# One feed-forward norm moved along the slots of an interleaved transformer stack

## The chip, the cores and the metric

The kernel runs on one core of a Trainium2 chip. The time is the device time of one execution in microseconds (us), the median of several runs. The core has five engines that work side by side, each through its own list of instructions in order: TensorE (PE in the profile; PEld is its weight loads), VectorE (DVE), ScalarE (ACT), GpSimd (POOL) and SyncE (SP, which here issues the DMA transfers). An instruction that needs another engine's result waits for a semaphore, and everything behind it on its engine waits too. Matmul results land in PSUM, of which this kernel's pools take eight banks of 128 x 512 floats.

## The reference

The computation is four residual blocks on x of 4 x 512 x 128: a linear attention, a stack of six transformer layers, another attention and a gated feed-forward. The change lies in the stack. One of its layers is:

```python
for i in range(DEPTH):                       # DEPTH = 6
    x = attn_layer(shift_tokens(x), Wqkv[i], q_scale[i], k_scale[i], Wo[i]) + x
    x = ffn_layer(shift_tokens(x), ln_g[i], ln_b[i], W1[i], b1[i], W2[i], b2[i]) + x

def ffn_layer(x, g, bln, W1, b1, W2, b2):
    mu = x.mean(-1, keepdims=True)
    var = ((x - mu) ** 2).mean(-1, keepdims=True)
    xn = (x - mu) / jnp.sqrt(var + 1e-05) * g + bln
    hg = xn @ W1 + b1
    a, gate = jnp.split(hg, 2, -1)
    return a * jax.nn.gelu(gate, approximate=False) @ W2 + b2
```

The attention has 16 heads of 64 and looks at windows of 32 queries and 64 keys; q and k are scaled to unit length and rotated. The feed-forward's hidden width is 341.

## The kernel before, in words

**Steps and slots.** The stack is cut into 48 steps: 6 layers x 4 batches (512 tokens each) x 2 halves of the heads (8 heads each). A step has four slots, one for each pair of heads, so there are 192 slots with scores, and some before and behind for filling and draining. The loop at the end of the stack runs over the slots `s`, and its body is a list written out by hand: each call appends its instructions to the engines' lists in just this order. In one slot the list has work of several steps at once: the scores of the present step (`here`), the projections of the step 2.5 steps ahead (`rot`), the transposes of k one step ahead (`turn`), the values half a step ahead (`val`), the weighted sums three slots behind and the output projection four slots behind (`back`).

**A plain slot, engine by engine.** TensorE: eight mask matmuls (L443) and 32 score matmuls (L453) into a pair of banks of which there is one; first projection of q or k (`pp`, L307); four transposes of k into a bank (`tp`, L387); output projection (L521); second projection (L307); weighted sums (L513); values (`pv`, L420). VectorE: maximum of the scores (L460) and `top` (L463), rotation products of the first projection (L318), sums of squares (L343), transposes of the probabilities (`blocks`, L488), products of the second projection, transpose of q (`qb`, L396), reciprocal (L478). ScalarE: four exponentials (L70, `pr`), square of the first projection (L329), copy of k's transposes (L388), four more exponentials, then copies of the weighted sums (L737) and values (L424) and the square of the second projection (L329). GpSimd: rotation sums (L339), normalised probabilities (L479), scaled k (L374), copies in place of the transposed probabilities (L502, L503). The next slot's scores may overwrite the score banks once the second four exponentials have read them.

**PSUM.** Three banks with the tag `mm` serve all of `pp`, `tp`, `pv` and the feed-forward's `pt`, `px`, `pg`, `pa` and `py`. They are handed out in the list's order, each to the next taker, as they come free. A projection's bank is free when both its readers, the rotation product (L318) and the square (L329), are done; the square is ordered behind the rotation product.

**The feed-forward.** It is cut into numbered parts, and a group (one layer, one batch) starts every eight slots. Part p of group g is due in slot `8 g + LATE[p - 1]`; `parts(s, (...))` in the list calls those of its parts that are due. There are 24 groups, g = 1 to 24. Slot numbers modulo 8 say therefore which parts a slot has:

- part 1 (L532): adds the attention's output to the residual stream z, on VectorE
- part 2 (L539, L543): four transposes of z into `pt`, copied by ScalarE to `xt`
- part 3 (L548 to L552): statistics of `xt`: four bn_stats, four bn_aggr, and the variance plus 1e-5 into `rs`, all on VectorE
- part 14 (L570 to L573): root and offset: `rs` to the power -0.5, and `off` as minus mean times `rs`, on GpSimd
- part 4 (L555): four products on ScalarE, `xt` times `rs` plus `off`, in place
- part 5 (L562, L564): four transposes of `xt` back into `px`, and gain and offset by ScalarE into `xg`
- part 6 (L578): gate matmuls into three banks `pg` and their gelu, which needs another table on ScalarE (loaded at L66)
- parts 7 and 8 (L589, L593): the other half of W1, times the gelu
- parts 9 and 15 (L599, L606): the matmuls with W2 into `py`, and their addition to z on VectorE
- parts 10 to 13: the residual of the whole block after the last layer

In slots with part 6 the copies L737 and L424 are made by VectorE and not by ScalarE.

Of the kernel before, what the change touches and what calls it, by code (L numbers as in the profile page):

```python
# [31 lines left out]
def sandwich(ctx: ExitStack, tc: tile.TileContext, a: dict, out: bass.AP):  # L32
# [254 lines left out]
    with tc.tile_pool(name="f0", bufs=2) as work, \  # L287
# [38 lines left out]
        def squares(k, j):  # L326
            o = proj[k]
            sq = o["sq"][j] = work.tile([P, S], F32, tag="ln_sd", name="sq")
            nc.scalar.activation(sq, o["pp"], AF.Square)  # L329
# [73 lines left out]
        def place_q(k, n):  # L403


            o = proj[k]
            if n == 0:
                o["qT"] = work.tile([P, 4, 4, 4, 32], F32, name="qT")
            for f in range(4):
                nc.sync.dma_start(  # L410
                    out=o["qT"][32 * f : 32 * f + 32, n], in_=o["qb"][32 * n : 32 * n + 32, f]
                )
# [21 lines left out]
        def score(k, p):  # L434


            o = proj[k]
            sc = scp.tile([P, 2, S], F32, tag="sc", name="sc")
            scores = o["sc"] = sc[:, :, 0 : 4 * KW].rearrange("p e (j k) -> p e j k", k=KW)
            for w in range(4):  # L440
                for e in range(2):
                    rows = slice(64 * e, 64 * e + 64)
                    nc.tensor.matmul(  # L443
                        sc[32 * w : 32 * w + 32, e, 0 : 4 * KW],
                        lhsT=identb[rows, 64 * e : 64 * e + 32], rhs=mask[rows, int(w == 0)],
                        start=True, stop=False, skip_group_check=True,
                    )
            for j in range(4):
                for w in range(4):
                    q0 = j * P + w * WIN  # L450
                    for e in range(2):
                        rows = slice(64 * e, 64 * e + 64)
                        nc.tensor.matmul(  # L453
                            scores[32 * w : 32 * w + 32, e, j, :],
                            lhsT=o["qT"][rows, w, p, j, :],
                            rhs=o["kT"][rows, p, q0 : q0 + KW],
                            start=False, stop=True, skip_group_check=True,
                        )
            raw = sc[:, 0, 4 * KW : 4 * KW + 8].rearrange("p (e j) -> p e j", e=2)
            nc.vector.tensor_reduce(raw, scores, AX.X, ALU.max, negate=True)  # L460
            top = o["top"] = work.tile([P, 2, 4], F32, name="top")
            o["rq"] = o["rn"][:, 0, :, 2 * p : 2 * p + 2]
            nc.vector.tensor_tensor(top, raw, o["rq"].rearrange("p j e -> p e j"), ALU.mult)  # L463
            o["pr"] = work.tile([P, 2, 4, KW], F32, name="pr")
            o["den"] = work.tile([P, 2, 4], F32, name="den")
# [54 lines left out]
        def output(i, c, t, py):  # L520
            nc.tensor.matmul(py, lhsT=ws[i]["wo"][:, c, :], rhs=t, start=(c == 0), stop=(c == 7))  # L521
# [1 line left out]


        ff = {}
        LATE = (3, 4, 4, 5, 7, 7, 8, 9, 13, 14, 15, 16, 17, 4, 13)

        def ff_part(i, b, part):
            w, zb = ws[i], z[b]
# [85 lines left out]
        def residual(b, part):  # L615
            if not res:
                t = wp.tile([P, 3 * S], F32, tag="wqkv0", name="res")
                res.update(y=t[:, 0:S], sd=t[:, S : 2 * S])
            y, sd = res["y"], res["sd"]
            if part == 1:  # L620
                for rows, cols in halves:
                    nc.gpsimd.tensor_copy(y[rows, :], z[b][rows, cols])
            elif part == 2:
                pc = mm.tile([P, S], F32, tag="mm", name="pc")
                nc.tensor.matmul(pc, lhsT=cent, rhs=y, start=True, stop=True)
                nc.scalar.activation(sd, pc, AF.Square)
                nc.vector.tensor_copy(y, pc)
            elif part == 3:
                pv = mm.tile([P, S], F32, tag="mm", name="pv")
                nc.tensor.matmul(pv, lhsT=mean_w, rhs=sd, start=True, stop=True)  # L630
                table_act(sd, pv, AF.Ln, bias=eps)
                table_act(sd, sd, AF.Exp, scale=-0.5)
            elif part == 4:
                nc.vector.tensor_tensor(y, y, sd, ALU.mult)
                nc.gpsimd.tensor_tensor(x[b], x[b], y, ALU.add)

        def inside(s, ahead):

            k, q = divmod(s + ahead, 4)
            return (k, q) if 0 <= k < len(steps) else None  # L640

        def parts(s, some):
            for part in some:
                g, left = divmod(s - LATE[part - 1], 8)
                if left or not 1 <= g <= DEPTH * NB:
                    continue
                if part < 10 or part > 13:
                    ff_part(*divmod(g - 1, NB), part)
                elif g > NB * (DEPTH - 1):
                    residual((g - 1) % NB, part - 9)  # L650
# [29 lines left out]
        with tc.manual_schedule():  # L680
            for s in range(-10, LAST + max(LATE) + 1):
                here, rot, before, flip = (inside(s, n) for n in (0, 10, 9, 9))
                fold, place, turn, val = (inside(s, n) for n in (6, 5, 4, 2))
                first = fold and fold[1] == 0

                copy = nc.scalar.copy
                if s % 8 == LATE[5] % 8 and LATE[5] < s:
                    copy = nc.vector.tensor_copy
                if place:
                    place_q(*place)  # L690
                if here:
                    score(*here)
                parts(s, (2, 5, 7, 8))
                if rot:
                    project(rot[0], 2 * rot[1])
                if here:
                    exponentials(here[0], 0)
                if rot:
                    rotate(rot[0], 2 * rot[1])
                    squares(rot[0], 2 * rot[1])  # L700
                if before:
                    squared(before[0], 2 * before[1] + 1)
                if turn:
                    turn_k(*turn)
                parts(s, (9,))
                back = inside(s, -4)
                if back:
                    i, b, hf = steps[back[0]]
                    c = 4 * hf + back[1]
                    if c == 0:  # L710
                        ff["py"] = pyp.tile([P, S], F32, name="py")
                    output(i, c, attn, ff["py"])
                if s - 1 in fresh:
                    by_keys[s - 1] = by_key(fresh.pop(s - 1))
                parts(s, (1, 3, 15))
                if s - 2 in by_keys:
                    in_place(*by_keys[s - 2])
                if rot:
                    squared(rot[0], 2 * rot[1])
                    rotated(rot[0], 2 * rot[1])  # L720
                if first:
                    guarded(fold[0])
                parts(s, (4,))
                if rot:
                    project(rot[0], 2 * rot[1] + 1)
                if here:
                    exponentials(here[0], 1)
                if first:
                    norms(fold[0])
                back = inside(s, -3)  # L730
                if back:
                    av = weighted(*back, by_keys.pop(s - 3)[0])
                if rot:
                    rotate(rot[0], 2 * rot[1] + 1)
                if back:
                    attn = work.tile([P, S], F32, tag="attn", bufs=1, name="attn")
                    copy(attn.rearrange("p (j h c) -> p j h c", j=4, h=2), av)  # L737
                if val:
                    value(*val, copy)
                if rot:  # L740
                    squares(rot[0], 2 * rot[1] + 1)
                if flip:
                    flip_q(*flip)
                if rot:
                    rotated(rot[0], 2 * rot[1] + 1)
                if here:
                    fresh[s] = normalise(here[0])
                if first:
                    refined(fold[0])
                if fold:  # L750
                    normed(*fold)
                parts(s, (14, 6, 10, 11, 12, 13))
                if here:
                    weights(*divmod(s, 32))
# [6 lines left out]
    with tc.tile_pool(name="f1w", bufs=1) as gp, tc.tile_pool(name="a1w", bufs=1) as wp, \  # L761
# [242 lines left out]
        parts = [(b, q, i) for b in range(NB) for q in range(2) for i in range(5)]  # L1004
# [195 lines left out]
```

## Time and profile before

| | us |
|---|---|
| median of 3 runs | 2001.5 (1999.19 to 2002.53) |
| the profiled execution | 2002.56 |
| its span, first to last instruction | 2000.9 |
| first scores of slot 0 | 127.5 |
| first scores of slot 191 | 1562.6 |

| engine | share of the span, busy |
|---|---|
| VectorE | 81% |
| ScalarE | 80% |
| GpSimd | 77% |

The stack is 72% of the span, and the granted TensorE clock in it is 1.00 (560 to 1500 us). Within that stretch of 940 us TensorE is busy for 916, VectorE for 841, GpSimd for 822 and ScalarE for 814 us: four engines are close to full. In such a kernel a share says little. What counts is which engine ends a slot, and that differs from slot to slot, since the feed-forward's parts fall into different slots. In the timeline rows the first number is the start in us from the start of the span, the second the length; `x4` after a row means that four instructions in a row are merged, and brackets give the engine's idle time before it and what ended it.

### The profile page before, as it was taken

To read this page: it belongs to the slowest core of one execution; us is meant where nothing else is said; L and a number is where in the kernel's file an instruction comes from. 1 tells how busy PE (TensorE), PEld (TensorE's weight loads), DVE (VectorE), ACT (ScalarE), POOL (GpSimd) and SP (SyncE) were. 2 spreads that over 40 slices of the span, in tenths; PEclk is the share of its full clock that TensorE was granted. 3 is DMA by queue.
4 is the path that set the end of the run, shared out by engine and by line. 5 is a ranking of instruction groups with operands and counts; after the bars stand their busy time and mean duration, and the time that the engine had idled before them with its cause. 6 is when DMAs were issued, how large, how long until landed. Compare 5 with 4: busy or idle time off the path is not lost.

```text
span 2000.9 us, 75927 instructions
## 1 busy us (share of the span) xinstructions
PE 1811.9 (91%) x30648; PEld 950.5 (48%) x30648; DVE 1625.4 (81%) x2561; ACT 1603.8 (80%) x4645; POOL 1547.9 (77%) x2026
## 2 busy tenths in 40 slices
PE   6779899999999999999999999999998868878868
PEld 3235455555555555555555555555555423323323
DVE  3698788888988888988888998889995369889833
ACT  3558788888888889888888888888888639989953
POOL 1289898888988889888898888888886338878850
PEclk8999999999999999999999999999999978889889
DMA  3023443344433444334434345333333110000000
GB/s 99 1 68 96 124 106 77 95 111 113 107 91 86 108 115 112 94 80 118 130 85 99 96 102 131 89 90 96 91 93 95 35 46 1 1 0 1 1 0 21
DMA packets 98892, 155.27 MB, mean 78 GB/s; under 512 B 29552, under 2 KB 56944, under 8 KB 93936
## 3 DMA queue, kind: packets, MB, share of 16 engines
q1 hardware_dynamic: 98544, 150.43, 29.5%
q8 instruction: 243, 3.98, 0.9%
q14 instruction: 105, 0.86, 0.2%
HBM read 23.44 MB, written 1.05 MB: 12 GB/s over the span
## 4 chain that ended last, share of the span: by engine, by line
PE 52%; DVE 16%; ACT 12%; POOL 7%; SPq 5%; issue 4%; DMA 3%; POOLq 0%; DVEq 0%; ACTq 0%
PE pp L307 10%; PE av L513 6%; PE pv L420 6%; PE sc L453 5%; PE py L521 5%; ACT pr L70 4%; PE pa L589 4%; PE pg L578 3%; DVE t L318 3%; DVE la L899 2%; DVE lb L897 2%; PE tp L387 2%; ACT xt L555 2%; POOL r L339 2%; ACT lb L70 2%
## 5 line engine op out<-in xcount | busy, mean ns | idle before, releaser
L70 ACT ACTIVATE pr<-sc,top,rn 128x64 f32<-128x64 f32 x1536 | 604.9, 415 | 99.8 <-DVE top L463 44.0
L339 POOL TENSOR_TENSOR r<-t 128x512 f32<-128x512 f32 x384 | 486.2, 1275 | 154.7 <-DVE t L318 134.2
L318 DVE TENSOR_TENSOR t<-pp,tab 128x1024 f32<-128x1024 f32 x384 | 467.9, 1219 | 39.5 <-PE pp L307 31.3
L307 PE MATMUL pp<-wqkv,z 128*128 128x512 f32 x768 | 410.6, 618 | 12.4 <-ACT sq L329 8.1
L70 ACT ACTIVATION_READ_ACCUMULATOR pr<-sc,top,rn 128x1 f32 x1536 | 329.6, 215 | 0.0
L329 ACT ACTIVATE sq<-pp 128x512 f32<-128x512 f32 x384 | 233.7, 609 | 89.3 <-DVE t L318 85.2
L343 DVE TENSOR_REDUCE ss<-sq 128x8 f32<-128x512 f32 x384 | 256.3, 668 | 3.4 <-ACT sq L329 1.1
L513 PEld LDWEIGHTS av<-pT,ve 64*64 64x64 f32 x6144 | 164.7, 134 | 154.5 <-POOL pT L502 46.4
L907 POOL TENSOR_TENSOR lb<-lb,la 128x2048 f32<-128x2048 f32 x40 | 182.5, 4563 | 53.2 <-issue 35.3
L420 PE MATMUL pv<-wqkv,z 128*128 128x512 f32 x384 | 217.0, 647 | 4.0 <-ACT sq L329 4.0
L479 POOL TENSOR_TENSOR pr<-pr,den 128x512 f32<-128x512 f32 x192 | 200.6, 1045 | 23.9 <-DVE den L478 23.8
L460 DVE TENSOR_REDUCE sc<-sc 128x8 f32<-128x512 f32 x192 | 131.4, 684 | 99.3 <-PE sc L453 98.7
L513 PE MATMUL av<-pT,ve 64*64 64x32 f32 x6144 | 197.0, 222 | 7.9 <-DMA qT<-qb 6.8
L374 POOL TENSOR_TENSOR r<-r,rn 128x512 f32<-128x512 f32 x192 | 200.3, 1043 | 3.8
L307 PEld LDWEIGHTS pp<-wqkv,z 128*128 128x128 f32 x768 | 134.1, 191 | 145.3 <-issue 106.4
L521 PE MATMUL py<-attn,wo 128*128 128x512 f32 x384 | 198.4, 598 | 1.5 <-ACT attn L737 1.5
L513 PE MATMUL av<-pT,vn 64*64 64x32 f32 x6144 | 193.2, 219 | 0.0
L453 PE MATMUL sc<-kT,qT 64*32 64x64 f32 x12288 | 171.1, 223 | 11.8 <-issue 11.8
L503 POOL COPY pT<-blocks 32x256 f32<-32x256 f32 x384 | 151.9, 396 | 22.3
L513 PEld LDWEIGHTS av<-pT,vn 64*64 64x64 f32 x6144 | 165.6, 135 | 0.2
L453 PEld LDWEIGHTS sc<-kT,qT 64*32 64x32 f32 x12288 | 154.6, 105 | 12.9 <-issue 12.7
L502 POOL COPY pT<-blocks 32x256 f32<-32x256 f32 x384 | 149.9, 390 | 11.0 <-issue 2.9
(195 smaller groups left out, 3270.4 us busy)
## 6 DMA issues: line engine op xcount, KB each, us to landing
qT<-qb SPq DMA_DIRECT2D x768, 64.0 KB
ve<-vn SPq DMA_DIRECT2D x48, 768.0 KB
pT<-blocks SPq DMA_DIRECT2D x768, 32.0 KB
wqkv<-in_f_wqkv SPq DMA_DIRECT2D x36, 256.0 KB
ve<-vn SPq DMA_DIRECT2D x48, 192.0 KB
tab<-in_rot SPq DMA_DIRECT2D x12, 256.0 KB
wo<-in_f_wo SPq DMA_DIRECT2D x6, 512.0 KB
ve<-vn SPq DMA_DIRECT2D x48, 64.0 KB
```

The source lines that it names most:

```text
L70: done = nc.scalar.activation(out, in_, func, **kw)
L307: nc.tensor.matmul(pp, lhsT=z[b][:, WIN + t * P : WIN + (t + 1) * P], rhs=ws[i]["qkv", hf][:, n * S : (n + 1) * S], start=True, stop=True,)
L318: nc.vector.tensor_tensor(t12, o["pp"].rearrange("p (h d) -> p h d", d=DH0).unsqueeze(1) .to_broadcast([P, 2, 8, DH0]), ws[i][f"tab{n}"][: ...
L329: nc.scalar.activation(sq, o["pp"], AF.Square)
L339: nc.gpsimd.tensor_tensor(r, t1, t2[:, :, ::-1, :], ALU.add)
L343: nc.vector.tensor_reduce(o["ss"][:, n, t, :], o["sq"].pop(j).rearrange("p (h d) -> p h d", d=DH0), AX.X, ALU.add,)
L374: nc.gpsimd.tensor_tensor(v, v, o["rn"][:, 1, t].unsqueeze(2).to_broadcast([P, 8, DH0]), ALU.mult)
L420: nc.tensor.matmul(pv, lhsT=z[b][:, WIN + t * P : WIN + (t + 1) * P], rhs=ws[i]["qkv", hf][:, 2 * S :], start=True, stop=True,)
L453: nc.tensor.matmul(scores[32 * w : 32 * w + 32, e, j, :], lhsT=o["qT"][rows, w, p, j, :], rhs=o["kT"][rows, p, q0 : q0 + KW], start=False, ...
L479: nc.gpsimd.tensor_tensor(o["pr"], o["pr"], o["den"].unsqueeze(3).to_broadcast([P, 2, 4, KW]), ALU.mult)
L513: nc.tensor.matmul(av[64 * e : 64 * e + 64, h, 64 * j + 32 * c : 64 * j + 32 * c + 32], lhsT=vs[c][rows, j, (2 * p + e) * DH0 : (2 * p + e ...
L521: nc.tensor.matmul(py, lhsT=ws[i]["wo"][:, c, :], rhs=t, start=(c == 0), stop=(c == 7))
```

## The change

Two parts of the feed-forward's norm get a later slot, four get another place in the list:

| part | slot modulo 8 | place in the list |
|---|---|---|
| 3, statistics | 4, now 5 | behind part 15 (was before it; 15 is due in this slot too) |
| 14, root and offset | 4, now 5 | unchanged: the end of GpSimd's list for the slot |
| 4, products | 5, now 6 | behind the square of the second projection, at the end of ScalarE's list for the slot; was ahead of the second projection and the second four exponentials |
| 5, transposes back and `xg` | 7, unchanged | behind k's transposes and part 9; was ahead of the first projection and the first four exponentials |

Nothing is added to the program or taken from it; the same instructions stand in another order. `xt` has one buffer, as before, and is now in use for one slot longer in its unscaled form.

```diff
-        LATE = (3, 4, 4, 5, 7, 7, 8, 9, 13, 14, 15, 16, 17, 4, 13)
+        LATE = (3, 4, 5, 6, 7, 7, 8, 9, 13, 14, 15, 16, 17, 5, 13)
...
-                parts(s, (2, 5, 7, 8))
+                parts(s, (2, 7, 8))
                 if rot:
                     project(rot[0], 2 * rot[1])
...
                 if turn:
                     turn_k(*turn)
-                parts(s, (9,))
+                parts(s, (9, 5))
...
-                parts(s, (1, 3, 15))
+                parts(s, (1, 15, 3))
...
                 if first:
                     guarded(fold[0])
-                parts(s, (4,))
                 if rot:
                     project(rot[0], 2 * rot[1] + 1)
...
                 if rot:
                     squares(rot[0], 2 * rot[1] + 1)
+                parts(s, (4,))
                 if flip:
                     flip_q(*flip)
```

## The prediction

> **What bounds the kernel now.** I read the page first: the busiest row, and then, since busy shares are averages, the list of waits and the timeline of one period of the stack.
>
> ```profile
> PE 1811.9 (91%) x30648; PEld 950.5 (48%) x30648; DVE 1625.4 (81%) x2561; ACT 1603.8 (80%) x4645; POOL 1547.9 (77%) x2026
> PE sc L443 <- ACT pr L70: 31.1, 46, 3.2
> ACT xt L555 <- POOL off L573: 21.7, 23, 3.1
> ```
>
> TensorE works 91% of the span. A slot, measured from the first mask matmul (L443) to the next slot's, has these medians over slots 24 to 183, by slot number modulo 8 ("class"): 7.12, 7.94, 6.24, 6.33, 7.35, 9.29, 6.22, 9.42 us for classes 0 to 7. A plain slot is 6.22 us of TensorE without a gap, so most slots are TensorE's own work. The second row is what is not: 46 times the next slot's scores wait for the exponentials (they reuse the one pair of score banks), 31.1 us in all, once in each class 4 and once in each class 5. That is the most the change could win from this wait.
>
> Class 5 first (slot 69, 647.78 to 657.06), ScalarE's timeline:
>
> ```profile
> 653.82 1.65 ACT L555 ACTIVATE xt<-xt,off,rs 128x128 f32<-128x128 f32 x4 [0.72 <-POOL off L573]
> 655.38 0.39 ACT L70 ACTIVATE pr<-sc,top,rn 128x64 f32<-128x64 f32 x1
> 656.90 0.58 ACT L737 COPY attn<-av 128x512 f32<-128x512 f32 x1
> ```
>
> The four products start only when GpSimd's root and offset are done (0.72 us idle), and the second four exponentials stand behind them: they end at 656.9, and the slot ends just after. TensorE alone would need 6.22 plus the six passes of L599, 2.58 (from 2.29 to 4.87 us in the slot): 8.80 us. The slot took 9.28.
>
> Now VectorE in slots 68 to 70:
>
> ```profile
> 645.73 0.83 DVE L548 BATCH_NORM_STATS2 st<-xt 128x6 f32<-128x128 f32 x4
> 646.88 0.31 DVE L552 TENSOR_SCALAR rs<-mv 128x4 f32<-128x4 f32 x1
> 647.09 0.67 DVE L343 TENSOR_REDUCE ss<-sq 128x8 f32<-128x512 f32 x1
> ...
> 648.82 0.69 DVE L396 STREAM_TRANSPOSE qb<-r 128x512 f32<-128x512 f32 x1
> 649.53 0.64 DVE L460 TENSOR_REDUCE sc<-sc 128x8 f32<-128x512 f32 x1
> ...
> 652.85 1.52 DVE L606 SCALAR_TENSOR_TENSOR z<-py,par,z 64x512 f32<-64x512 f32 x2
> 656.26 0.70 DVE L396 STREAM_TRANSPOSE qb<-r 128x512 f32<-128x512 f32 x1
> 658.06 0.70 DVE L460 TENSOR_REDUCE sc<-sc 128x8 f32<-128x512 f32 x1 [0.81 <-PE sc L453]
> ```
>
> The statistics take 1.36 us of VectorE (645.73 to 647.09). Because of them VectorE enters class 5 with old work: its transpose starts 1.04 us into the slot and the score maximum at 1.75 us. In class 6, where it enters in step, the maximum starts at 1.00 us, after a wait for the scores.
>
> Last, class 7 (slot 71, from 663.28), ScalarE and TensorE:
>
> ```profile
> 664.57 0.61 ACT L329 ACTIVATE sq<-pp 128x512 f32<-128x512 f32 x1
> 665.05 0.79 ACT L564 ACTIVATE xg<-px,par 128x512 f32<-128x512 f32 x1
> 665.84 0.41 ACT L70 ACTIVATE pr<-sc,top,rn 128x64 f32<-128x64 f32 x1
> 667.38 0.60 ACT L329 ACTIVATE sq<-pp 128x512 f32<-128x512 f32 x1
> 664.18 0.66 PE L562 MATMUL px<-ident,xt 128*128 128x128 f32 x4
> 666.13 1.02 PE L521 MATMUL py<-attn,wo 128*128 128x512 f32 x2
> 666.99 1.02 PE L307 MATMUL pp<-wqkv,z 128*128 128x512 f32 x2
> 672.70 0.30 PE L443 MATMUL sc<-mask,identb 64*32 64x256 bf16 x8
> ```
>
> ScalarE has no gap from the end of slot 70's exponentials through these rows, yet TensorE never waits: its second projection (666.99, that is 3.71 us into the slot) needs the PSUM bank that px had, and this is free when xg is done, 2.56 us into the slot.
>
> **The change, part by part.** Each of the 24 feed-forward groups passes once. Of these 23 lie in slots with attention work, the last in the tail.
>
> *Class 4: the statistics leave, 0.* They stand on VectorE behind the maximum. The stall at this slot's end comes from the late maximum, and that from the residual addition (L532) in class 3, which stays.
>
> *Class 5: the products leave, -0.5.* Without them and with VectorE in step, the second exponentials end near 6.2 us, and TensorE sets the slot: 9.28 to 8.80, -0.48; with the class's mean of 9.37 the gain is 0.57. I take 0.5.
>
> *Class 6: the statistics arrive late, +0.65.* They now stand behind L606, which waits for L599, so they cannot start before 6.6 us. What follows moves by 1.36: slot 69's transpose from 8.48 to 9.84 us, in a slot of 8.80, so 1.04 us into class 6. That is the lateness that class 5 has today (648.82 in a slot from 647.78). The maximum then starts at 1.75 and not 1.00 and carries the exponentials with it; they end close to the slot's end today, so the scores of class 7 wait for them. Of 0.75 about 0.1 is slack. Behind the maximum wait both sets of exponentials, and behind these the next scores. The ends are 0 (VectorE catches up) and 0.75.
>
> Here a rule bears on the price. The SBUF page of the Trainium skill ("SBUF — State Buffer", section "Who interferes with whom") has VectorE and GpSimd share a port pair as an exclusive lock: a tensor_scalar in its two-port form waits for GpSimd's whole instruction. The trace agrees:
>
> ```profile
> 662.11 1.03 DVE L351 TENSOR_SCALAR ss<-ss 128x64 f32<-128x64 f32 x1
> 661.82 1.27 POOL L339 TENSOR_TENSOR r<-t 128x512 f32<-128x512 f32 x1
> ```
>
> Both end near 663.1, and L351 is 0.18 us in class 2, where GpSimd isn't in its way. L552 moves with the statistics and has 0.17 to 1.27 us. By its row (median 0.31) it costs what I charged; by the rule's worst case, behind an L339, 1.1 us more, 25 us in all. It should run about 7.7 us into class 5. There GpSimd, rid of root and offsets, should have ended its first rotation sum (today from 655.57, 7.79 us into the slot; less 1.55, plus 1.25 of its own: 7.5) and wait for VectorE's next product; so I take the row.
>
> *GpSimd's root and offsets, 0.* About 1.5 us (652.21 to 653.76) move from behind class 5's to behind class 6's normalisations. Attention's in-place copies behind them serve the next slot's L513, and end about 0.5 us into class 7, where L513 comes after 4.66 us even today. The rotation sums become about 1 us later; the next product on VectorE still finds its buffer free. No DMA is issued by any moved part; SP's queue keeps its order, and its transposes' producers move with their slots.
>
> *Class 7: products ahead of the exponentials, transposes behind k's, +1.82.* The products now follow L329 at the end of class 6's list on ScalarE, in time 1.77 us into class 7 (665.05). Four take 1.56 (653.82 to 655.38). The first exponentials start at 3.33 instead of 2.56, take 1.54 (665.84 to 667.38), and the square of the slot's first projection starts at 4.87. The three general PSUM banks go round, and the fourth taker in a slot gets the first taker's bank. Before, the takers are px, pp, tp, then pp; now pp, tp, px, then pp. So the second projection waits no longer for xg but for that square. In the changed program's instruction list this is the wait it carries. From a square's start to the matmul that waits for it takes 0.66 us:
>
> ```profile
> 137.64 0.60 ACT L329 ACTIVATE sq<-pp 128x512 f32<-128x512 f32 x1
> 138.30 1.12 PE L420 MATMUL pv<-wqkv,z 128*128 128x512 f32 x2 [0.87 <-ACT sq L329]
> ```
>
> So the projection starts at 5.53 instead of 3.71: +1.82, and behind it are L513, L420 and the gate matmuls, all in order. Nothing else is later: px ends by 3.6, output L521 by 4.5, xg (now behind kT) by 6.6, while the gate matmuls come at 8.5; the second exponentials end at 8.15 in a slot of 11.2. The following slots don't give it back; class 0 and 1 are TensorE's own time. Where class 7 starts late anyway (mean 9.63, median 9.42) part is absorbed: -0.15.
>
> *Tail, +3.4.* In the last group nothing is beside the chain. The statistics ended at 1588.36; now they stand behind L606, which ends at 1590.50, plus 1.36: 1591.86.
>
> Sum: 23 x (-0.5 + 0.65 + 1.82 - 0.15) = 23 x 1.82 = 41.9, plus 3.4: +45 us on the profiled execution's 2002.6, so 2047.6. That execution lies 1.1 above the median of 2001.5; forecast **2046.5 us**.
>
> **Rivals.** (a) *The bank is free*: the second projection meets no square, only px's wait. px then ends at 3.58, L521 0.86 later, the projection at 4.44: +0.73 in place of +1.82, and in all 23 x (-0.5 + 0.65 + 0.73 - 0.15) + 3.4 = +20, 2021.5 with the 1.1 to the median. For it: banks could come free in another order; against it: the order of takers above. (b) *Faster*: the class 5 wait goes, and ScalarE takes the products in idle time: 23 x -0.5 + 3.4 = -8, 1993.5. It decides where ScalarE has 1.6 us idle before class 7's first exponentials; there must also be no lateness in class 6. For it are the 0.72 us idle before L555 now; against it the gapless rows from 663.17 on. (c) *VectorE blocked* at L552 in most periods: +25, 2071. (d) *No change*: class 6 at 0 and the bank free make 23 x (-0.5 + 0.73 - 0.15) + 3.4 = +5; with 0.2 us of px's wait hidden too, 2001.5.
>
> **How the numbers follow.** Forecast 0.74, (a) 0.13, (b) 0.06, (c) 0.04, (d) 0.03. Class 6 at 0 gives 2031, class 7 at half its price 2026; class 6 at 0.75 with nothing absorbed gives 2052, and half of (c) on top 2064. With (a) inside, the range is 2018 to 2064; (b), (c) and (d), 0.13, are left out. A difference of 0.2%, 4 us, is about what a measurement here can tell from none. Slower holds forecast, (a) and (c): 0.91; faster 0.06, same 0.03.
>
> **What would show it.** Class 5 at 8.8; class 6 at 6.9 with the maximum at 1.75; class 7 near 11.2, with L307's second start at 5.5 and a wait of PE pp L307 for ACT sq L329, some 0.7 to 1 us in each period, new in the list; "ACT xt L555 <- POOL off" gone. A class 7 that stays below 10 would make it wrong.

## The result, and the profile after

The changed kernel takes 2031.8 us (2028.6 to 2034.7, four runs) where the kernel before, measured beside it, takes 2000.4: a ratio of 1.0164, interval 1.0137 to 1.019. It is 31.5 us, or 1.6%, slower. The profiled execution of the changed kernel took 2028.59 us with a span of 2026.7, so 26 more than the profiled execution of before; it is the shortest of its four runs.

The medians of the slots by class, as in the prediction, over slots 24 to 183:

| class | 0 | 1 | 2 | 3 | 4 | 5 | 6 | 7 |
|---|---|---|---|---|---|---|---|---|
| before, us | 7.12 | 7.94 | 6.24 | 6.34 | 7.35 | 9.29 | 6.22 | 9.42 |
| changed, us | 7.12 | 7.94 | 6.25 | 6.35 | 7.27 | 8.80 | 6.84 | 11.20 |

Three classes differ: one gains half a microsecond and two lose. The busy row and the waits of the changed kernel (who waits, for which tile and line, on whom; us in total, times, the longest) show the causes:

```profile
PE 1823.1 (90%) x30648; PEld 949.8 (47%) x30648; DVE 1618.8 (80%) x2561; ACT 1605.1 (79%) x4645; POOL 1548.7 (76%) x2026
...
PEld pp L307 <- ACT sq L329: 56.2, 38, 2.3
PE sc L443 <- ACT pr L70: 32.9, 52, 2.2
PE pp L307 <- ACT sq L329: 23.1, 27, 1.5
ACT xt L555 <- POOL off L573: 7.5, 1, 7.5
```

The engines' work is what it was: their busy times moved by less than 1%. The wait of L555 for GpSimd, once 23 times, is left in one place, the tail. The wait of L443 for the exponentials is as large as before, 52 times instead of 46: it left the end of class 5 (21 times before, none now) and came up at the end of class 6 (3 times before, 23 now). And the projection L307, whose weight load (PEld) and matmul (PE) waited before for the square L329 19 and 9 times, 21.7 and 8.1 us, now does so 38 and 27 times.

**Class 7** (slot 71, from 661.88 us), timeline of the changed kernel, TensorE:

```profile
661.88 0.30 PE L443 MATMUL sc<-mask,identb 64*32 64x256 bf16 x8 [0.40 <-ACT pr L70]
...
662.77 1.12 PE L307 MATMUL pp<-wqkv,z 128*128 128x512 f32 x2
663.73 0.60 PE L387 MATMUL tp<-ident,r 128*128 128x128 f32 x4
664.16 1.46 PE L562 MATMUL px<-ident,xt 128*128 128x128 f32 x4
665.46 1.02 PE L521 MATMUL py<-attn,wo 128*128 128x512 f32 x2
667.33 1.12 PE L307 MATMUL pp<-wqkv,z 128*128 128x512 f32 x2 [0.84 <-ACT sq L329]
...
673.08 0.30 PE L443 MATMUL sc<-mask,identb 64*32 64x256 bf16 x8
```

and ScalarE in the same slot:

```profile
663.60 1.64 ACT L555 ACTIVATE xt<-xt,off,rs 128x128 f32<-128x128 f32 x4
665.14 0.40 ACT L70 ACTIVATE pr<-sc,top,rn 128x64 f32<-128x64 f32 x1
...
666.67 0.61 ACT L329 ACTIVATE sq<-pp 128x512 f32<-128x512 f32 x1
```

Products 1.72 us into the slot, exponentials at 3.26, square at 4.79, and 0.66 us after the square's start the second projection, at 5.45. The bracket names what ended TensorE's idle time: the square, and not px or its copy. The 1.46 of L562 is no longer work; its four transposes follow the four products as they come.

**Classes 5 and 6** (slots 69 and 70, from 646.24 and 655.04), VectorE of the changed kernel:

```profile
651.31 1.52 DVE L606 SCALAR_TENSOR_TENSOR z<-py,par,z 64x512 f32<-64x512 f32 x2 [0.51 <-PE py L599]
652.85 0.87 DVE L548 BATCH_NORM_STATS2 st<-xt 128x6 f32<-128x128 f32 x4
...
654.04 0.17 DVE L552 TENSOR_SCALAR rs<-mv 128x4 f32<-128x4 f32 x1
...
655.97 0.70 DVE L396 STREAM_TRANSPOSE qb<-r 128x512 f32<-128x512 f32 x1
...
656.68 0.65 DVE L460 TENSOR_REDUCE sc<-sc 128x8 f32<-128x512 f32 x1
```

VectorE idles 0.51 us ahead of L606 with the statistics ready behind it, then does L606 and the statistics one after the other. Class 5's last transpose (L396) falls 0.93 us into class 6, and the maximum (L460) starts at 1.64.

### The profile page after: what moved, and what is told of

It reads as the page before. It is cut to its first block, busy times and chain, and to the rows that moved or that the text cites. A ratio compares the mean times of both kernels' runs of the same rounds, so it can differ in the third digit from the quotient of the medians.

```text
span 2026.7 us, 75946 instructions
## 1 busy us (share of the span) xinstructions
PE 1823.1 (90%) x30648; PEld 949.8 (47%) x30648; DVE 1618.8 (80%) x2561; ACT 1605.1 (79%) x4645; POOL 1548.7 (76%) x2026
## 4 chain that ended last, share of the span: by engine, by line
PE 43%; ACT 23%; DVE 19%; SPq 4%; issue 4%; DMA 3%; POOL 2%; DVEq 0%; ACTq 0%; POOLq 0%
ACT pr L70 10%; PE pp L307 8%; PE av L513 4%; PE pv L420 4%; DVE t L318 4%; PE sc L453 4%; PE pa L589 3%; PE pg L578 3%; PE py L599 3%; ACT sq L329 3%; ACT lb L70 3%; PE py L521 3%; DVE la L899 2%; DVE lb L897 2%; DVE ss L343 2%
## 5 line engine op out<-in xcount | busy, mean ns | idle before, releaser
L339 POOL TENSOR_TENSOR r<-t 128x512 f32<-128x512 f32 x384 | 485.8, 1275 | 178.2 <-DVE t L318 163.5
L307 PE MATMUL pp<-wqkv,z 128*128 128x512 f32 x768 | 413.2, 621 | 28.8 <-ACT sq L329 23.1
L70 ACT ACTIVATION_READ_ACCUMULATOR pr<-sc,top,rn 128x1 f32 x1536 | 333.7, 217 | 0.0
L329 ACT ACTIVATE sq<-pp 128x512 f32<-128x512 f32 x384 | 236.4, 616 | 92.6 <-DVE t L318 91.7
L513 PEld LDWEIGHTS av<-pT,ve 64*64 64x64 f32 x6144 | 163.7, 134 | 150.1 <-issue 34.9
L460 DVE TENSOR_REDUCE sc<-sc 128x8 f32<-128x512 f32 x192 | 132.0, 687 | 103.4 <-PE sc L453 102.9
L307 PEld LDWEIGHTS pp<-wqkv,z 128*128 128x128 f32 x768 | 132.3, 191 | 169.3 <-issue 102.1
L513 PE MATMUL av<-pT,ve 64*64 64x32 f32 x6144 | 196.5, 222 | 3.7 <-DMA qT<-qb 3.2
L521 PE MATMUL py<-attn,wo 128*128 128x512 f32 x384 | 197.7, 597 | 1.5 <-ACT attn L736 1.5
L513 PE MATMUL av<-pT,vn 64*64 64x32 f32 x6144 | 192.4, 219 | 0.0
L513 PEld LDWEIGHTS av<-pT,vn 64*64 64x64 f32 x6144 | 164.7, 135 | 0.0
```

Of the source, the lines that this page charges most:

```text
L70: done = nc.scalar.activation(out, in_, func, **kw)
L307: nc.tensor.matmul(pp, lhsT=z[b][:, WIN + t * P : WIN + (t + 1) * P], rhs=ws[i]["qkv", hf][:, n * S : (n + 1) * S], start=True, stop=True,)
L339: nc.gpsimd.tensor_tensor(r, t1, t2[:, :, ::-1, :], ALU.add)
L513: nc.tensor.matmul(av[64 * e : 64 * e + 64, h, 64 * j + 32 * c : 64 * j + 32 * c + 32], lhsT=vs[c][rows, j, (2 * p + e) * DH0 : (2 * p + e ...
```

## The experiments

The wait had two possible causes (the order of the bank's takers, or the products ahead of the exponentials), and class 6 a cause of its own. The first four runs part them; e1, e2 and e3 undo or do one piece, e4 keeps everything and moves what the bank's reader stands behind. The kernel before ran beside each lot: 1996.7 us with e1 to e4, 1997.4 with e5 to e8, so runs of different lots are compared by their ratios.

**e1, the transposes alone.** Only part 5 moves behind k's transposes; statistics and products stay.

```diff
-                parts(s, (2, 5, 7, 8))
+                parts(s, (2, 7, 8))
...
-                parts(s, (9,))
+                parts(s, (9, 5))
```

> Only the transposes back and xg move, to behind k's transposes, as in the change; statistics, root and products stay in classes 4 and 5. Theory (the fourth taker's bank): the second projection of class 7 now waits for the first projection's square although no product lies ahead of the exponentials. VectorE is late in class 7 (its maximum starts at 1.62 us), so the first exponentials start near 2.5, the square near 4.05, the projection 0.66 later at 4.7 instead of 3.71: class 7 near 10.4 instead of 9.42, +1.0 in each period, about +22 us in all. Class 5 stays at 9.3, class 6 at 6.2. Rival (only the wait for the products costs, not the bank): class 7 stays at 9.4, time as before.

Measured: 2022.7 us, ratio 1.0114 (1.0074 to 1.0154). Class 7 has a median of 10.53, class 5 stays at 9.28. TensorE in its slot 71, which starts at 665.98:

```profile
668.71 1.02 PE L521 MATMUL py<-attn,wo 128*128 128x512 f32 x2
670.75 1.12 PE L307 MATMUL pp<-wqkv,z 128*128 128x512 f32 x2 [1.02 <-ACT sq L329]
```

No products lie in this slot, L521 is done early, and the projection waits all the same, for the square, until 4.77 us. So the place in the list by itself gives the projection the bank that the first projection had. ScalarE shows why it isn't earlier still:

```profile
667.26 0.61 ACT L329 ACTIVATE sq<-pp 128x512 f32<-128x512 f32 x1
668.56 0.40 ACT L70 ACTIVATE pr<-sc,top,rn 128x64 f32<-128x64 f32 x1 [0.68 <-PE tp L387]
...
670.09 0.60 ACT L329 ACTIVATE sq<-pp 128x512 f32<-128x512 f32 x1
```

The square stands behind the first four exponentials, and these come 2.58 us into the slot, when VectorE's maximum is there (`top` ends 0.12 us before; the tp in the bracket had long been done). ScalarE idles 0.68 us here because the maximum is late, 1.62 us into the slot; in the changed kernel it starts at 1.09 and the four products, 1.6 us, lie ahead of the exponentials. So these come only 0.68 later than in e1, and class 7 is 11.20 instead of 10.53.

**e2, the products alone.** Part 4 goes to the end of the next slot, the transposes stay ahead of the first projection.

```diff
-        LATE = (3, 4, 4, 5, 7, 7, 8, 9, 13, 14, 15, 16, 17, 4, 13)
+        LATE = (3, 4, 4, 6, 7, 7, 8, 9, 13, 14, 15, 16, 17, 4, 13)
...
-                parts(s, (4,))
...
                     squares(rot[0], 2 * rot[1] + 1)
+                parts(s, (4,))
```

> Only the products move, to the end of class 6's list; statistics stay in class 4, transposes back stay at the head of class 7. Theory: class 5 falls to 8.8, class 6 stays at 6.2; in class 7 the transposes wait at the head of TensorE's list until the products end at 3.4 us, and all behind them with them: first projection at 3.5 instead of 1.45, class 7 near 11.5. Sum about +37 us. It shows whether moving the transposes behind k's, taken by itself a loss, softens this one: the change's class 7 is 11.2. Rival (the transposes' place doesn't matter beside the products): class 7 at 11.2 here too.

Measured: 2029.0 us, ratio 1.0159 (1.0118 to 1.02), 32 us where 37 were expected; class 5 at 8.80, class 6 at 6.24, class 7 at 11.44. Here the transposes, first in TensorE's list after the scores, wait for the products, and all projections wait behind them. So the late products alone cost class 7 2.02, the late transposes alone 1.11, and both together 1.78: the sum isn't additive, and the new place of the transposes saves 0.24 of what the late products cost in class 7. In slot 71 the wait cost something more (start in us, then name and matmuls; the slot starts at 663.25 and takes 12.98):

```profile
665.52 1.62 PE L562 MATMUL px<-ident,xt 128*128 128x128 f32 x4 [1.31 <-ACT xt L555]
666.93 1.91 PE L307 MATMUL pp<-wqkv,z 128*128 128x512 f32 x2
```

L307 takes 1.91 instead of 1.12: the granted clock was 0.5 for a while. This is taken up at the end.

**e3, the statistics back.** The changed kernel with parts 3 and 14 in class 4 again.

```diff
-        LATE = (3, 4, 5, 6, 7, 7, 8, 9, 13, 14, 15, 16, 17, 5, 13)
+        LATE = (3, 4, 4, 6, 7, 7, 8, 9, 13, 14, 15, 16, 17, 4, 13)
```

> The changed kernel with statistics and root back in class 4. Theory (class 6's loss is VectorE's lateness from statistics behind the residual addition): class 6 returns from 6.84 to 6.2, class 5 stays at 8.8, class 7 at 11.2, and the tail gives back its 3 us: about 16 us below the changed kernel, some +15 on the kernel before. Rival (class 6 is late through GpSimd's root and offset or through the products at its end): class 6 stays near 6.8 in one of these cases, since the products remain at its end; the time falls by under 5 us.

Measured: 2017.0 us, ratio 1.0101 (1.0063 to 1.0139); class 5 at 8.80, class 6 at 6.24, class 7 at 11.20, the tail 436.7. VectorE in slot 70 (from 654.92):

```profile
655.92 0.70 DVE L460 TENSOR_REDUCE sc<-sc 128x8 f32<-128x512 f32 x1 [0.54 <-PE sc L453]
```

VectorE again waits for the scores, 1.00 us into the slot, where in the changed kernel it arrived at 1.64 without waiting. Class 6's loss goes with that lateness and not with the products, which stay at its end; class 7 and class 5 don't move with it. The root and offset on GpSimd went back too, so e3 doesn't part them from the statistics; e6 does. The time is 13 us below the changed kernel by the ratios, where 16 were expected, and 20 above the kernel before, where 15 were.

**e4, the square first.** The changed kernel, but in class 7 the first exponentials stand behind the square.

```diff
-                if here:
+                if here and s % 8 != 7:
                     exponentials(here[0], 0)
...
                     squares(rot[0], 2 * rot[1])
+                if here and s % 8 == 7:
+                    exponentials(here[0], 0)
```

> The changed kernel, but in class 7 ScalarE squares the first projection before the first four exponentials. Theory (the second projection waits for the square and not for the products): the square starts when the products end, near 3.3, and the projection is held only by the transposes' wait for the last product and L521 behind it: 4.4 instead of 5.45; class 7 near 10.2. Exponentials and gelu end 0.5 later, so class 0 may rise by up to 0.4. About 15 to 24 us below the changed kernel. Rival (the projection is held by the products through the transposes alone): class 7 stays at 11.2.

Measured: 2021.2 us, ratio 1.013 (1.0083 to 1.0176); class 7 has 10.29, class 0 7.17. In slot 71 (from 664.36) the square follows the products at once and the projection starts 4.45 us into the slot, without a wait:

```profile
666.08 1.64 ACT L555 ACTIVATE xt<-xt,off,rs 128x128 f32<-128x128 f32 x4
667.78 0.60 ACT L329 ACTIVATE sq<-pp 128x512 f32<-128x512 f32 x1
668.28 0.40 ACT L70 ACTIVATE pr<-sc,top,rn 128x64 f32<-128x64 f32 x1
...
668.81 1.02 PE L307 MATMUL pp<-wqkv,z 128*128 128x512 f32 x2
```

Of class 7's +1.78 this gives back 0.91 in the median, close to the 1.0 expected. In the mean it is 0.72 and 0.80 against the two profiles of the changed kernel: slots 23, 47, 63, 127 and 167, in which TensorE stood still for 0.6 to 1.2 us (see the end), are 0.6 to 1.1 over the median now that no wait behind takes this in. The time shows less: 7 us below the changed kernel by the ratios, with overlapping intervals, where 15 to 24 were expected; so it is the slots and not the time that show the cause. The exponentials, now behind the square, delayed the next slot by 0.05 in the median and not by the 0.4 that had been set down as the most. What remains against before is TensorE's L562 waiting for the products, and class 6.

**e5, the products in an idle stretch.** Not the change, but its other idea done elsewhere: from before, the products move by a few lines only, behind the second four exponentials of class 5.

```diff
-                parts(s, (4,))
                 if rot:
                     project(rot[0], 2 * rot[1] + 1)
                 if here:
                     exponentials(here[0], 1)
+                parts(s, (4,))
```

> The kernel before with one edit: the products stay in class 5 but stand behind the second four exponentials instead of ahead of them. There ScalarE has nothing to do until the weighted sums are ready (in the changed kernel it is idle for 1.65 us of class 5). Theory: the exponentials end near 6.9, class 5 falls from 9.29 to 8.8 and no other class changes, since the products are done by 8.4 us, before the next slot's work on ScalarE: about -12 to -15 us. Rival (products at any later place push the copies L737 and L424 behind them and with them the next slot): class 6 rises by some 0.3 and the gain is halved.

Measured: 1980.1 us, ratio 0.99 (0.9865 to 0.9936), faster than both kernels. Class 5 is 8.80 like in the changed kernel, and class 6 (6.23) and class 7 (9.36) are as before. ScalarE in slot 69 (640.03 to 648.91):

```profile
646.37 0.45 ACT L70 ACTIVATE pr<-sc,top,rn 128x64 f32<-128x64 f32 x1
...
646.76 1.67 ACT L555 ACTIVATE xt<-xt,off,rs 128x128 f32<-128x128 f32 x4
648.30 0.61 ACT L737 COPY attn<-av 128x512 f32<-128x512 f32 x1
```

The exponentials end at 646.8, 2.1 us before the next scores, so the score banks are free in time; of the copies that are now late, L737 serves the next slot's L521 and frees the bank for its L513. The gain of 17 us between the medians is above the 12 to 15 expected. The profiled execution is 20 us shorter than that of before: class 5's sum over the whole stack is 15.6 of it, class 3's 2.0, the tail 1.2 and classes 4, 6 and 7 together 1.5, all but the first of the size of what changes between runs.

**e6, the statistics ahead of the addition.** The changed kernel with its parts 3 and 15 in the old order.

```diff
-                parts(s, (1, 15, 3))
+                parts(s, (1, 3, 15))
```

> The changed kernel with the statistics ahead of the addition L606 in class 5. Theory (class 6's price is VectorE's lateness, and it can be dosed): VectorE is idle for 0.5 us before L606 today; the statistics fill this, so what follows is late by some 0.85 instead of 1.36 us; class 6's maximum starts near 1.2 instead of 1.64, class 6 near 6.4 instead of 6.84, and the tail loses its 3 us: about 12 us below the changed kernel. Rival (another engine makes class 6 late): class 6 stays at 6.84.

Measured: 2020.1 us, ratio 1.0106 (1.0069 to 1.0144); class 6 has 6.27 (mean 6.38), class 7 11.20, the tail 439.2. VectorE in a slot of class 5, and then the maximum of the slot behind it, which starts at 660.49:

```profile
656.17 0.83 DVE L548 BATCH_NORM_STATS2 st<-xt 128x6 f32<-128x128 f32 x4
...
657.32 0.17 DVE L552 TENSOR_SCALAR rs<-mv 128x4 f32<-128x4 f32 x1
657.39 1.51 DVE L606 SCALAR_TENSOR_TENSOR z<-py,par,z 64x512 f32<-64x512 f32 x2
...
661.50 0.69 DVE L460 TENSOR_REDUCE sc<-sc 128x8 f32<-128x512 f32 x1
```

The statistics now fill the time in which VectorE waited for L599, and the maximum starts at 1.01. GpSimd's root and offset stay late here and class 6 is short all the same, so they are not what costs it 0.6; nor is it class 5 as such, but the place behind a waiting instruction. Two numbers in a list are worth 12 us by the ratios (1.0106 against 1.0164), and 15 against e8, which ran beside it.

**e7, a second stall besides.** e5's edit, and q's transpose of class 3 is held until the next slot's scores, to make class 4's maximum early.

```diff
+            held = None
             for s in range(-10, LAST + max(LATE) + 1):
...
                     score(*here)
+                if held:
+                    flip_q(*held)
+                    held = None
...
-                if flip:
+                if flip and s % 8 == 3 and s > 0:
+                    held = flip
+                elif flip:
                     flip_q(*flip)
```

> The same edit of the kernel before (products behind the second exponentials), and in class 3 the transpose of q (L396) is held back and done in class 4, behind the maximum. Theory (class 4's end comes from a late maximum, which the change left as it was): the maximum of class 4 starts at 1.5 instead of 2.2, the exponentials end some 0.5 earlier, class 4 falls from 7.35 to 6.85; with class 5 at 8.8 about -24 us against the kernel before. Rival (class 4 is held by ScalarE's own queue, not by the maximum): class 4 stays at 7.3, and the time is that of the single edit.

Measured: 1985.6 us (thirteen runs, 1976.8 to 1994.8), ratio 0.993 (0.9906 to 0.9955): no better than e5, and not the 24 us less that were expected. Class 4's median fell only to 7.10, half of the forecast. ScalarE in slot 68 (from 630.68):

```profile
632.81 0.58 ACT L543 COPY xt<-pt 128x512 f32<-128x512 f32 x1
633.27 0.42 ACT L70 ACTIVATE pr<-sc,top,rn 128x64 f32<-128x64 f32 x1
```

The maximum was early, at 1.57, but the first exponentials came at 2.59 us, behind ScalarE's copy of `xt` (L543), which stands ahead of them; and class 5's mean rose to 9.07 from e5's 8.87. The stall of class 4 wants another cure.

**e8, the changed kernel again**, to see what of its profile repeats.

> The changed kernel once more, for a second profile of it. Theory: medians of the classes as in the first (8.80, 6.84, 11.20 for classes 5 to 7); the irregular stalls of class 3, a part of the sum that I had not forecast, fall differently, so the mean of class 3 is not a result of the change. Rival (class 3 gained 0.2 us through the change): class 3's mean is again 6.58 or below.

Measured: 2035.5 us, ratio 1.0175 (1.0134 to 1.0217). The medians of all classes are the same within 0.08, and those of classes 5, 6 and 7 equal; class 3's mean is 6.70, between the 6.58 of the first profile and the 6.80 before, so half of class 3's gain did not come again.

## Why the prediction was right, step by step

The mechanism was the one forecast, in each place that the sum names; the size was 45 us forecast on the profiled execution, against 26 and 34 in two profiled executions and 31.5 between the medians. The sums over slots 0 to 190 and the spans, each profile less that of before:

| us | forecast | changed | again (e8) |
|---|---|---|---|
| class 5 | -11.5 | -17.6 | -17.3 |
| class 6 | +15.0 | +12.5 | +11.7 |
| class 7, with what it absorbs | +38.4 | +32.4 | +34.0 |
| class 3 | 0 | -6.2 | -4.3 |
| classes 0, 1, 2 and 4 | 0 | +1.0 | +3.8 |
| ahead of slot 0 | 0 | -2.3 | +0.7 |
| tail (from the scores of slot 191) | +3.4 | +6.1 | +4.2 |
| sum | +45.3 | +25.9 | +32.8 |

In four rows the forecast was too high: class 5 gained 6 us more than forecast, class 7 lost 4 to 6 less and class 6 about 3 less, and class 3's 4 to 6 are mostly chance. Without class 3 the two profiles miss the forecast by 13 and 8 us.

*Class 4, 0.* Right: 7.27 and 7.35 in the two profiles of the changed kernel, 7.35 before. The stall there is the late maximum's, and e7 shows that it is also ScalarE's copy.

*Class 5, -0.5.* The median did as said, 9.29 to 8.80, and e2, e3 and e5 show that moving the products alone does it: in these three the statistics stand in class 4, so VectorE being in step, which the prediction also asked for, isn't needed. The term was too small where it counted, in the sum: slots that stood out before lost more. Slot 13, in the filling of the stack, went from 9.49 to 6.41; it has no L599 yet, so nothing there hid the products. Slot 21 went from 10.13 to 8.83. The mean over slots 24 to 183 fell by 0.65. The prediction's means, 9.37 for class 5 and 9.63 for class 7, don't belong to the slots of its medians; over slots 24 to 183 they are 9.46 and 9.54. The first would have given 9.46 less 8.80, or 0.66, where 0.5 was taken. Nor are the 46 waits of L443 one in each class 4 and class 5: the trace has 17 at the end of class 4, 21 at the end of class 5 with 14.0 us, and 8 elsewhere.

*Class 6, +0.65.* Right in size (+0.61) and cause (e3, e6). The maximum came at 1.64 where 1.75 was set. In the sum 21 periods carry it and not 23: slot 14, in the filling, and slot 190, the last, lose nothing.

*L552 by its row and not by the lock's worst case.* Right: its median fell from 306 to 170 ns. In the changed kernel's slot 69 it starts at 654.04, 7.80 us into the slot, and GpSimd's rotation sum L339 had run from 652.02 to 653.29 and waits. Where L552 did start beside an L339 it took long: 1.27 us in slot 172 before, 0.81 in slot 13 of the changed kernel, and each ended within 0.03 us of that L339. The rule of the Trainium skill that was weighed there ("SBUF — State Buffer", "Who interferes with whom") agrees with these traces.

The same collision changed where the prediction did not look, on L351, whose row it quotes. In class 6 before, L351 took 1.03 us in the median of slots 30 to 182; in the changed kernel it takes 0.18. In slot 70 it now starts when GpSimd's root (L570) has just ended, and no L339 runs:

```profile
660.43 0.18 DVE L351 TENSOR_SCALAR ss<-ss 128x64 f32<-128x64 f32 x1
659.37 1.02 POOL L570 TENSOR_TENSOR rs<-rs,mhalf 128x4 f32<-128x4 f32 x1
```

L351 is as short in e2 to e7, which all take the products from ahead of the second exponentials in class 5, and 1.03 in e1, which doesn't. The maximum of class 7 starts 1.62 us into its slot where L351 is long, in before and e1, and at 1.00 to 1.11 in the eight others (medians). The changed kernel's exponentials gain nothing by it, as they stand behind the products until 3.26.

*GpSimd, 0.* No wait for root and offsets is left in the stack. That its later rotation sums cost nothing is not shown by a run of its own; e3, which takes them back together with the statistics, puts classes 5 and 7 where the changed kernel has them.

*Class 7, +1.82.* Right in cause and median: +1.78, with products, exponentials, square and projection each within 0.08 us of its forecast time. e1 shows the bank's part of it without the products, e4 that the square is what the projection waits for. The price that rival (a) gave to px's wait alone was right too: it put the projection at 4.44 us, and e4, where the square holds nothing up, has it at 4.45. As a whole rival (a), a free bank, and (d) are out by e1; (b), faster, is out for this place of the products, and e5 shows the place where it holds. The term that failed is the count, "23 x": slot 191 has no projections, since those run ten slots ahead, and slot 183 has none either and lost 1.19. Of what class 7 lost, 21 periods carry the full price less what is absorbed. Slot 23 absorbed all of it: it had stalled to 11.29 before and took 11.20. The mean change over slots 24 to 183 was +1.62 and +1.69, so the 0.15 for absorption was well sized.

*Class 3 and the filling*, not in the forecast. Class 3's mean lay between 6.51 and 6.81 in the ten profiles, and e3, whose class 3 is ordered like the changed kernel's, has 6.81. So most of the -6.2 is chance, not the change; it makes 2 of the 7 us between the two profiles' sums, and the stretch ahead of slot 0 makes 3. Part of it is slot 11, in which the products of no group stand: 11.74 before, 9.85 and 8.84 in the changed kernel, and from 8.20 (e7) to 12.40 (e4) in all. TensorE stands still there before its first L513, for 4.0 us before, 3.2 and 2.2 in the changed kernel and 1.6 to 4.1 in all ten; the profile names the landing of a DMA as what ended it. In before and e1 to e6 the granted clock also fell to 0.5 in that slot, for 3.4 or 6.8 us; in the changed kernel's profiles and e7 it did not. Why that landing varies stays open.

*Tail, +3.4.* 6.1 and 4.2 (the prediction's own figures, 1588.36 and 1591.86, give 3.5). The statistics' place behind L606 makes it: the three profiles that have it take 441.7 to 444.4 us from the scores of slot 191, the seven others 436.7 to 439.2, in the mean 4.6 less.

## What to carry to other kernels

Where tiles of one tag go round a few banks, the place of an operation in the list decides whose release it meets: count the takers, and look behind which work the last reader of that bank stands (here a square behind four exponentials, 1.1 us per period for the transposes' move alone). Work that is taken out of an engine's critical stretch must go where that engine is idle, and that can be a few lines away in the same slot: behind the exponentials it gained 17 us, one slot later, in a stretch without gaps, it lost 32 (e2). And what is ready goes ahead of what waits: the order of two parts on one engine was worth 12 to 15 us.

## What the runs showed of the hardware

A wait of TensorE can cost more than its length. In e2 the granted clock fell to 0.5 for 3.4 us at 294.5, 666.5, 1161.5 and 1472.1 us, each time in a slot of class 7 (23, 71, 135, 175) in which TensorE had stood idle for the products, and these four took 1.5 to 1.6 us more than their class; it fell once more in slot 183, of class 7 too. The windows of e2 around the second (stretch, length, busy time and instructions of PE, PEld, DVE, ACT and POOL, granted clock, DMA share, GB/s):

```profile
663.30:665.50 2.20, 0.90 (x73) 0.74 (x72) 1.64 (x5) 2.17 (x7) 2.20 (x3) 1.00 0.68 183
665.50:669.50 4.00, 3.83 (x11) 2.12 (x12) 0.55 (x1) 3.43 (x12) 3.59 (x9) 0.63 0.28 62
```

TensorE is busy for 0.9 of the first 2.2 us; then 1.00 becomes 0.63 over four. Most slots of class 7 have the same idle time and keep their clock, so it is not the length alone that decides. The changed kernel's own wait, 0.84 us and ahead of dense matmuls, set off none in the stack, in either profile.

TensorE also stands still now and then with nothing to wait for, within the score matmuls: in before 0.7 to 1.2 us at slots 67, 107 and 147 of class 3 and 47, 127 and 167 of class 7, and 1.8 at slots 23 and 43. The six are 20 slots apart or a multiple, and e8 has them again in all six and in slot 87, with 1.0 to 2.1 us; the first profile of the changed kernel has fewer. In class 7 of the changed kernel the wait for the square takes most of them in: of e8's four there only slot 87 was over 0.5 longer than its class, and in it the granted clock fell to 0.5 for 3.4 us, 0.9 us after the stall. Such a fall came behind a stall of 1.8 to 2.1 us in e1 (slots 147 and 167), e3 (147) and e4 (43) too, but none behind the 1.8 us in slot 127 of e3. What the stalls are the trace doesn't say; it names no releaser.
